# The seam between the mixing and the last part: image 0's spectra loaded early, its last two columns copied from evicted tiles, and a fixed order

## The chip, the cores and the metric

The kernel runs on one core of a Trainium2 chip. The metric is the device time of one launch in microseconds (us), the median of several runs. Engines are named as in the profile: PE (matmuls), PEld (PE's weight loads), DVE (vector), ACT (scalar), POOL (GpSimd) and SP (the sync engine, which here only issues DMAs). A trailing q, as in SPq, is the part of an engine that issues DMAs.

## What is computed

All data is float32. The input is 32 images of 128 channels, 64 x 64 pixels. A convolution in a learned transform domain comes first, then attention over channels and a mixture of experts on the pixels as tokens. Cut to what matters:

```python
x = x + conv(group_norm(x))
# conv: x_f = tensor_product(x)            butterflies along h and w, complex
#       prod = einsum('bihw,oihw->bohw', x_f, w_f)
#       out = real(tensor_product_inverse(prod))
t = tokens(x)                              # 4096 tokens of 128 channels per image
t = t + attn(layer_norm(t))                # softmax of a 128 x 128 channel Gram matrix
t = t + moe(layer_norm(t))                 # 8 experts, top 2, gates renormalised
x = from_tokens(t)
```

## The kernel before

The work has three parts, one after another.

Part one (lines 163 to 563) goes over the 32 images: group norm, and the two butterflies as matmuls with 64 x 64 matrices. Its results, the spectra, go to the DRAM tile `xf`.

Part two (lines 566 to 757), the mixing, goes over the 64 columns w of the spectrum. For each w, SP loads the column of all images and input channels in four tiles `l` (pool `lp`, a ring of 8), POOL spreads them into the tile `s` (lines 600 and 602), PE makes the weights' spectrum `g` from `wst` (line 632), ACT and DVE bring it to `f` (643), and PE multiplies `s` with `f` (654, the tiles `m`). ACT and DVE evict `m` into one of two tiles `o`, one for each half of the 64 + 64 output channels (`mix_out`, line 664; its last argument hh picks ACT or DVE, and the DVE copy comes after the ACT one). `store` (line 673) writes a half of column w into the DRAM tile `pf`, in eight DMAs of 128 KB on SP. A tile `o` holds column w in the partitions of w % 2, so after the last column it holds columns 62 and 63.

Part three (lines 763 to 1390) goes over the images again. For image b, eight tiles `r` (pool `rp`, a ring of 10) are loaded from `pf`, each with 16 output channels, all 64 columns, real part in partitions 0 to 63 and imaginary part in 64 to 127 (`load_r`, line 856: two DMAs of 256 KB). PE applies the inverse transform along w. For the first two images this is done in 16 pieces per image (`pw`, line 920, evicted by ACT into `u` at 927), for the later ones in eight (`pu`, 877). Then follows the inverse along h (`pz`, 939, or `py`, 899), which DVE adds to the image `y` (947 or 907), which is loaded from the input again. Then come the transposition to tokens (`pt`, 1021), layer norm, attention and experts (`pe`, 1296), and the store. In the steady state the steps of three images overlap.

The order of the instructions on each engine comes from a planner (`Plan`, line 25): each operation is given an engine, an estimated duration, a due time, what it follows and which buffers of a ring it takes and frees. The planner plays this through and then emits the operations in the order it found. Within `tc.manual_schedule()` that order is kept; the code between the second and the third planner's run (lines 763 to 797: pools, loads of constants, clearing `rank`) is outside of it, and the framework's own scheduler places it. When a pool's memory is taken over by a new pool, a tile in it waits for what used that memory before.

At the seam of parts two and three the third part's list `first` is emitted ahead of its planner's operations: `prepare` (line 799), which folds a mean into the expert weights, the attention weights and the router's column sums by four PE products (804, 812, 820) with DVE work behind each, and then `load_r` of image 0 for e = 0 and 1 on POOL and for e = 2 and 3 on ACT. `prepare` reads `wkv`, `prx` and `kvb`, which ACT's queue loads (lines 774 to 797). The other four tiles `r` of image 0 and its image `y` are loaded on SP.

Of the kernel before, what the change touches and what calls it, by code (L numbers as in the profile page):

```python
# [10 lines left out]
F32 = mybir.dt.float32  # L11
# [3 lines left out]
PSUM = bass.MemoryType.PSUM  # L15

P = 128
HW = 64
NPIX = HW * HW
NT = NPIX // P  # L20
NE = 8
# [69 lines left out]
def kernel(  # L91
# [15 lines left out]
    nc = tc.nc  # L107
    B = x.shape[0]
    xv = x.rearrange("b c h w -> b c (h w)")
# [3 lines left out]
    n = HW  # L113
# [6 lines left out]
    pf = dram.tile([n, n, P * n], F32, name="pf")  # L120
# [35 lines left out]
    nc.gpsimd.memset(mhalf, -0.5)  # L156

    wctx = ctx.enter_context(ExitStack())
    wstp = wctx.enter_context(tc.tile_pool(name="wstp", bufs=1))
    wst = wstp.tile([P, 32, P], F32, name="wst")  # L160


    with ExitStack() as ph1:
        pp = ph1.enter_context(tc.tile_pool(name="pp1", bufs=4, space=PSUM))
        xp = ph1.enter_context(tc.tile_pool(name="xp1", bufs=3))
        st = ph1.enter_context(tc.tile_pool(name="st1", bufs=1))
# [19 lines left out]
        lo, hi = slice(0, n), slice(n, P)  # L186
# [244 lines left out]
        def store(b, g):  # L431
            def run():
                f = tile_of.pop(("f", b, g))

                for k in range(0, 8, 4):
                    nc.sync.dma_start(xf[b, :, 8 * g + k : 8 * g + k + 4, :], f[:, k : k + 4])
            return run
# [125 lines left out]
            plan.run()  # L563


    with ExitStack() as ph2:
        gp = ph2.enter_context(tc.tile_pool(name="gp", bufs=2, space=PSUM))
        mp = ph2.enter_context(tc.tile_pool(name="mp", bufs=2, space=PSUM))
        lp = ph2.enter_context(tc.tile_pool(name="lp", bufs=8))
        sp = ph2.enter_context(tc.tile_pool(name="sp", bufs=2))  # L570
        wf = ph2.enter_context(tc.tile_pool(name="wf", bufs=2))
        op = ph2.enter_context(tc.tile_pool(name="op", bufs=1))
# [95 lines left out]

        def store(w, half):

            for c in range(0, n, 8):
                lo = (half * n + c) * n
                nc.sync.dma_start(
                    pf[w, :, lo : lo + 8 * n], outs[half][w % 2 * n : w % 2 * n + n, c : c + 8].rearrange("m o h -> m (o h)")
                )

        rest = []
# [21 lines left out]
        def mixed(*after):  # L699

            while rest:
                w, half, g, at = rest.pop()
                add(
                    ("mo", w, half, g, 1), "DVE", 1.25, at + 0.1, lambda: mix_out(w, half, g, 1),
                    [("mo", w, half, g, 0), *after], (), ("m",),
                )
                if g:
                    add(
                        ("st", w, half), "SP", 0.1, at + 0.2, lambda: store(w, half),
                        [("mo", w, half, g, hh) for g in range(2) for hh in range(2)], (), ("o",), 8.0,  # L710
                    )

# [50 lines left out]
    eps = ctx.enter_context(tc.tile_pool(name="eps", bufs=3, space=PSUM))  # L763
    cps = ctx.enter_context(tc.tile_pool(name="cps", bufs=1, space=PSUM))
    tps = ctx.enter_context(tc.tile_pool(name="tps", bufs=3, space=PSUM))
    rp = ctx.enter_context(tc.tile_pool(name="rp", bufs=10))
    xp = ctx.enter_context(tc.tile_pool(name="xp", bufs=2))
    st = ctx.enter_context(tc.tile_pool(name="st", bufs=1))
    up = ctx.enter_context(tc.tile_pool(name="up", bufs=1))
    wp = ctx.enter_context(tc.tile_pool(name="wp", bufs=2))  # L770
    pfv = pf.rearrange("w (r b) (e m) -> b e r w m", r=2, e=8)
    ct = ctx.enter_context(tc.tile_pool(name="ct", bufs=1))
    wkv = ct.tile([P, 2, P], F32, name="wkv")
    nc.scalar.dma_start(wkv[:, 0, :], wkT)
    nc.scalar.dma_start(wkv[:, 1, :], wvT)
    rb_sb = ct.tile([P, NE], F32, name="rb_sb")
    nc.scalar.dma_start(rb_sb, router_b.partition_broadcast(P))


    rank = ct.tile([P, NE], F32, name="rank")  # L780
# [6 lines left out]
    QX = P + 2 * NE  # L787
    prx = [ct.tile([P, QX], F32, name=f"prx{i}") for i in range(2)]
    for t in prx:
        nc.scalar.dma_start(t[:, P + NE : QX], router_w)  # L790
    rws = ct.tile([P, NE], F32, name="rws")

    tk = [ct.tile([P, NT, P], F32, name=f"tk{i}") for i in range(2)]
    u = up.tile([P, n, P], F32, name="u")
    kvb = ct.tile([P, 2, P], F32, name="kvb")
    nc.scalar.dma_start(kvb[:, 0, :], bk.partition_broadcast(P))
    nc.scalar.dma_start(kvb[:, 1, :], bv.partition_broadcast(P))

    def prepare():

# [41 lines left out]
            engine, us, SLOT * at, run, [made[k] for k in names if k[0] >= 0], take, free, late  # L842
        )

    xs, rs, tile_of, first = {}, {}, {}, [prepare]

    def transfers(b):
        def load_x():
            xs[b] = xp.tile([P, HW, HW], F32, tag="x", name=f"y{b}")
            nc.sync.dma_start(xs[b].rearrange("c h w -> c (h w)"), xv[b])  # L850

        def load_r(e, queue=nc.sync):
            def run():
                t = rs[b, e] = rp.tile([P, 16 * n], F32, tag="r", name=f"r{b}_{e}")
                for r in range(2):
                    queue.dma_start(t[r * n : (r + 1) * n], pfv[b, e, r])
            return run

        if b == 0:

            first.extend(load_r(e, nc.gpsimd if e < 2 else nc.scalar) for e in range(4))

        for e in range(8):
            early = b == 0 and e < 4
            add(
                b, f"r{e}", "SP", 0.2, b - 0.5 + 0.08 * e, (lambda: None) if early else load_r(e), take=("r",),
                late=0.0 if early else 5.0,
            )
        add(b, "x", "SP", 0.1, b + 0.2, load_x, take=("x",), late=12.0)

    def conv(b):
        def w_inverse(e):
# [71 lines left out]
        def h_out_piece(q):  # L944
            def run():
                acc = xs[b][:, :, 8 * q : 8 * q + 8]
                nc.vector.tensor_tensor(
                    acc, tile_of.pop(("cz", b, q)).rearrange("o (w h) -> o h w", h=n), acc, ALU.add
                )
            return run  # L950

        if b < 2:
            for e in range(8):
                at = b + 0.08 * e
                for oh in range(2):
                    add(
                        b, f"w{e}_{oh}", "PE", 0.95, at + 0.04 * oh, w_inverse_piece(e, oh),
                        [f"r{e}"] + [(b - 1, f"h{k}") for k in range(4)], ("pe",), ("r",) if oh else (),
                    )
                    add(  # L960
                        b, f"wo{e}_{oh}", "ACT", 0.65, at + 0.04 * oh, w_out_piece(e, oh), [f"w{e}_{oh}"], (), ("pe",),
                    )
            for g in range(4):
                for k in range(2):
                    at = b + 0.68 + 0.07 * g + 0.035 * k
                    h, ho = (f"h{g}", f"ho{g}") if k else (f"h{g}_0", f"ho{g}_0")
                    add(
                        b, h, "PE", 1.05, at, h_inverse_piece(2 * g + k),
                        [f"wo{e}_{oh}" for e in range(8) for oh in range(2)] + ([f"h{g}_0"] if k else []), ("pe",),
                    )  # L970
# [411 lines left out]
    for b in range(B):  # L1382
# [1 line left out]
        conv(b)  # L1384
        front(b)
        experts(b)
    with tc.manual_schedule():
        for run in first:
            run()
        plan.run()  # L1390


# [51 lines left out]
```

## Time and profile before

| | |
|---|---|
| three runs | 6056.81, 6056.97, 6062.2 us; median 6056.97 |
| span of the profiled execution | 6062.4 us (0.2 above the highest of the three runs; 5.4 above the median) |
| busy: PE, PEld | 5891.6 us (97%), 4677.6 us (77%) |
| busy: DVE, ACT, POOL | 4221.2 us (70%), 3756.5 us (62%), 4191.0 us (69%) |
| part one, part two, part three | to about 931, 931 to 2537, from 2537 us on |
| one image in the steady state of part three | 106.4 us |
| instructions fetched | queue q8: 749 packets, 12.27 MB |
| time to landing: `pf<-o`, `r<-pf` on SP, POOL, ACT | 3.3, 4.7, 7.3, 10.7 us (medians) |

A line of the timeline has the start and the length in us, the engine, the line of the kernel, the operation with the tiles it writes and reads, the count, and in brackets the idle time of the engine ahead of it with what ended that. "issue" means that the engine waited for nothing that the profile shows. The chain of waits goes back from the last instruction of the kernel, at each step to what released it. A line of the table by stretches has the stretch, its length, and the busy time (with the number of instructions) of PE, PEld, DVE, ACT and POOL, then the clock granted to PE as a share of the full one, the busy share of the 16 DMA engines and what they moved in GB/s.

### The profile page before, as it was taken

What the parts mean: (1) busy time and instruction counts of PE and PEld (TensorE: products, weight loads), DVE (VectorE), ACT (ScalarE), POOL (GpSimd) and SP (SyncE); (2) the same over time, 40 slices, a digit from 0 to 9 for tenths busy, and PEclk for the clock granted to TensorE, in tenths of its full rate; (3) what the DMA queues carried; (4) which work ended last, traced back from release to release, by engine and by line L of the source; (5) the groups of instructions that cost most, each with busy time, mean ns of one, the idle gap of its engine ahead of it and who ended that gap; (6) DMA issues with size and microseconds to landing.
All of it is one profiled execution on the core that took longest, in us unless ns stands there. A gap on an engine that the chain in (4) does not pass through costs nothing.

```text
span 6062.4 us, 219265 instructions
## 1 busy us (share of the span) xinstructions
PE 5891.6 (97%) x95372; PEld 4677.6 (77%) x95372; DVE 4221.2 (70%) x7696; ACT 3756.5 (62%) x7057; POOL 4191.0 (69%) x3765
## 2 busy tenths in 40 slices
PE   7999999999999999889999999999999999999998
PEld 7999999999999999776666666666666666666654
DVE  5565545555555555448878787787878878787878
ACT  7666664555555555366667667666766766676663
POOL 2110006666666666428898898989989898998988
PEclk9999999999999999999999999999999999999999
DMA  6767666666666666632313222231322223132100
GB/s 200 238 224 237 234 214 193 172 173 172 172 174 171 171 171 172 160 107 77 92 56 102 67 88 81 72 97 57 101 68 84 84 64 104 57 97 71 65 27 28
DMA packets 555044, 756.74 MB, mean 125 GB/s; under 512 B 58592, under 2 KB 319712, under 8 KB 549984
## 3 DMA queue, kind: packets, MB, share of 16 engines
q1 hardware_dynamic: 551856, 738.76, 41.0%
q8 instruction: 749, 12.27, 0.9%
q0 software_dynamic: 896, 2.62, 0.1%
q14 instruction: 215, 1.76, 0.1%
q10 hardware_dynamic: 1328, 1.32, 0.1%
HBM read 406.93 MB, written 335.54 MB: 122 GB/s over the span
## 4 chain that ended last, share of the span: by engine, by line
PE 88%; ACT 7%; issue 2%; DVE 1%; POOL 1%; DMA 1%; SPq 0%; ACTq 0%; POOLq 0%; DVEq 0%
PE pe L1296 28%; PE m L654 17%; PE g L632 9%; PE pf L418 7%; PE pu L877 6%; PE pp L1145 4%; PE py L899 4%; PE pg L1072 4%; PE pv L396 3%; PE px L1283 2%; ACT xn L1273 2%; ACT u L887 2%; PE pz L373 1%; PE pt L1021 1%; ACT z L383 1%
## 5 line engine op out<-in xcount | busy, mean ns | idle before, releaser
L1296 PE MATMUL pe<-ew_sb,xT 128*128 128x512 f32 x4096 | 1948.4, 597 | 18.6 <-DVE tm L1307 15.1
L1307 DVE TENSOR_TENSOR tm<-pe,oh 128x512 f32<-128x512 f32 x2028 | 1346.6, 684 | 478.9 <-PE pe L1296 456.6
L1332 POOL TENSOR_TENSOR tm<-tm 128x512 f32<-128x512 f32 x1014 | 1285.0, 1284 | 202.6 <-DVE tm L1307 199.3
L1296 PEld LDWEIGHTS pe<-ew_sb,xT 128*128 128x128 f32 x4096 | 701.6, 191 | 523.4 <-issue 400.1
L643 DVE COPY f<-g 128x1024 f32<-128x1024 f32 x508 | 622.3, 1225 | 644.4 <-PE g L632 644.2
L654 PE MATMUL m<-f,s 128*64 128x64 f32 x32768 | 1068.9, 224 | 1.1 <-ACT f L643 0.8
L654 PEld LDWEIGHTS m<-f,s 128*64 128x64 f32 x32768 | 999.0, 138 | 62.4 <-issue 1.5
L600 POOL COPY s<-l 128x512 f32<-128x512 f32 x512 | 547.2, 1105 | 526.4 <-issue 509.7
L643 ACT COPY f<-g 128x1024 f32<-128x1024 f32 x508 | 514.7, 1013 | 556.4 <-PE g L632 530.1
L1335 POOL TENSOR_TENSOR tk<-tk,tm 128x256 f32<-128x256 f32 x1014 | 753.9, 743 | 79.5
L1333 POOL TENSOR_TENSOR tm<-tm 128x512 f32<-128x512 f32 x507 | 650.3, 1283 | 39.8
L887 ACT COPY u<-pu 64x512 f32<-64x512 f32 x960 | 556.3, 579 | 135.1 <-PE pu L877 121.6
L632 PE MATMUL g<-c,wst 9*128 9x128 f32 x16256 | 599.6, 283 | 1.7 <-issue 1.5
L632 PEld LDWEIGHTS g<-c,wst 9*128 9x128 f32 x16256 | 503.0, 186 | 36.2 <-issue 1.5
L349 POOL TENSOR_TENSOR grstd<-gms,mhalf 128x1 f32<-128x1 f32 x32 | 17.8, 555 | 737.8 <-DVE gms L345 737.8
L1158 ACT ACTIVATE pp<-pp,m 128x128 f32<-128x128 f32 x1024 | 440.9, 431 | 124.2 <-PE pp L1145 99.2
L602 POOL TENSOR_SCALAR s<-l 128x512 f32<-128x512 f32 x256 | 511.3, 1997 | 0.0
L877 PEld LDWEIGHTS pu<-qw,r 128*128 128x128 f32 x3840 | 455.1, 193 | 62.8 <-ACT u L887 49.0
L877 PE MATMUL pu<-qw,r 128*128 128x128 f32 x3840 | 475.8, 277 | 25.1 <-ACT u L887 25.1
L1289 ACT COPY xT<-px 128x512 f32<-128x512 f32 x256 | 150.2, 587 | 563.2 <-PE px L1283 560.1
L418 PE MATMUL pf<-ph,v 128*128 128x128 f32 x4096 | 491.2, 278 | 6.2 <-issue 1.4
L418 PEld LDWEIGHTS pf<-ph,v 128*128 128x128 f32 x4096 | 467.0, 192 | 16.0 <-ACT z L383 7.1
(169 smaller groups left out, 8569.6 us busy)
## 6 DMA issues: line engine op xcount, KB each, us to landing
xf<-f SPq DMA_DIRECT2D x512, 256.0 KB, 3.3
pf<-o SPq DMA_DIRECT2D x1024, 128.0 KB, 3.3
l<-xf SPq DMA_DIRECT2D x1012, 128.0 KB, 3.2
r<-pf SPq DMA_DIRECT2D x504, 256.0 KB, 4.7
x<-in_x_dram SPq DMA_DIRECT2D x256, 256.0 KB, 4.5
y<-in_x_dram SPq DMA_DIRECT2D x32, 2048.0 KB, 9.3
out_dram<-so SPq DMA_DIRECT2D x256, 256.0 KB, 2.2
tw<-in_tw_dram SPq DMA_DIRECT2D x6, 384.0 KB, 7.5
```

Source lines behind the costliest of these rows:

```text
L418: nc.tensor.matmul(pl[:, j * P : (j + 1) * P], vs[b][:, 8 * g + j, :], ph.rearrange("h r m -> h (r m)"), start=True, stop=True,)
L600: nc.gpsimd.tensor_copy(dst, src)
L632: nc.tensor.matmul(pg[g // 2][:, g % 2, m * P : (m + 1) * P], wst[rows, 16 * half + 4 * t + m, :], c[rows].rearrange("r h k -> r (h k)"), ...
L643: copy(f.rearrange("i m (g o) -> i m g o", g=2), tile_of["g", w, half, t][k].rearrange("i g (o m) -> i m g o", o=4))
L654: nc.tensor.matmul(ps[hh * n : (hh + 1) * n, q, :], s[:, h].rearrange("i k b -> i (k b)")[:, B * r : B * r + n], f[:, h, r, :], start=(r = ...
L877: nc.tensor.matmul(ps[:, k, :], rs[b, e][:, k * P : (k + 1) * P], qw.rearrange("w r m -> w (r m)"), start=True, stop=True,)
L887: nc.scalar.copy(u[r * n : (r + 1) * n, :, oh * n + 8 * e : oh * n + 8 * e + 8], ps[oh * n : (oh + 1) * n, :, r * n : (r + 1) * n].rearran ...
L1296: nc.tensor.matmul(ps, tile_of["xT", b, i // 4][:, i % 4, :], ew_sb[:, es, :].rearrange("d e c -> d (e c)"), start=True, stop=True,)
L1307: nc.vector.tensor_tensor(tile_of["tm", b, i // 2][:, i % 2, es, :], tile_of.pop(("pe", b, i, half)).rearrange("p (e c) -> p e c", c=P), t ...
L1332: nc.gpsimd.tensor_tensor(tm[:, k, 0:4, :], tm[:, k, 0:4, :], tm[:, k, 4:8, :], ALU.add)
L1333: nc.gpsimd.tensor_tensor(tm[:, :, 0:2, :], tm[:, :, 0:2, :], tm[:, :, 2:4, :], ALU.add)
L1335: nc.gpsimd.tensor_tensor(t[:, lo : lo + 2, :], t[:, lo : lo + 2, :], tm[:, :, m, :], ALU.add)
```

## The change

- The ring of part three's tiles `r` is opened ahead of part two (pool `rp`, now 8 tiles) and serves part two as the ring of the tiles `l` too; two more tiles come from a pool `rp2` in part three. Tile i = 8b + e lies in `rp` where i % 10 < 8.
- At the end of part two POOL loads rows 0 to 61 of all eight tiles `r` of image 0 from `pf` (`first_rows`: 16 DMAs of 62 rows of 4 KB). They follow the stores of column 61 and POOL's last spread.
- Rows 62 and 63 of each half come from the tiles `o` in SBUF (`last_rows`: 16 DMAs of two rows on SP), when the halves of columns 62 and 63 are evicted; all 16 stand on SP ahead of the store of the second half of column 63.
- The store of the first half of column 63 goes from SP to POOL. Behind it on POOL stand the load of image 0's `y`, all loads of constants (from ACT) and the clearing of `rank`.
- `prepare` becomes an operation of the third planner, behind the last `pz` of image 0; on PE its four products come between the last `pz` and the first `pt`, and on DVE its six instructions come ahead of the last addition to `y` of image 0. The first pieces `pw` of image 1 come later among the `pt` of image 0: the first stood ahead of all of them and comes behind the fifth.
- The fixed order spans everything from part two on. The pools of part three reuse memory with waits by tile, and their order is changed; `wst` and the constants lie on the other side of the memory.

Apart from this, the order of the instructions on each engine is the same in both kernels.

```diff
-    wstp = wctx.enter_context(tc.tile_pool(name="wstp", bufs=1))
+    wstp = wctx.enter_context(tc.tile_pool(name="wstp", bufs=1, side="right"))
...
+    rp = ctx.enter_context(tc.tile_pool(name="rp", bufs=8))
+    pfv = pf.rearrange("w (r b) (e m) -> b e r w m", r=2, e=8)
+    ctx.enter_context(tc.manual_schedule())
+    rs = {}
     with ExitStack() as ph2:
...
-        lp = ph2.enter_context(tc.tile_pool(name="lp", bufs=8))
...
-            t = tile_of["l", w, j] = lp.tile([P, NB, 2, n], F32, tag="l", name=f"l{w}_{j}")
+            t = rp.tile([P, 16 * n], F32, tag="r", name=f"l{w}_{j}")
+            t = tile_of["l", w, j] = t.rearrange("i (b r h) -> i b r h", b=NB, r=2)
...
         def store(w, half):
+            queue = nc.gpsimd if (w, half) == (n - 1, 0) else nc.sync
...
+        def first_rows(e):
+            t = rs[0, e] = rp.tile([P, 16 * n], F32, tag="r", name=f"r0_{e}")
+            for r in range(2):
+                nc.gpsimd.dma_start(t[r * n : r * n + n - 2], pfv[0, e, r][0 : n - 2])
+
+        def last_rows(e):
+            half, lo = e // 4, 16 * (e % 4)
+            for r in range(2):
+                nc.sync.dma_start(
+                    rs[0, e][r * n + n - 2 : r * n + n],
+                    outs[half][B * r : B * r + n + 1 : n, lo : lo + 16].rearrange("m o h -> m (o h)"),
+                )
...
+        for e in range(8):
+            half = e // 4
+            add(("r", e), "POOL", 1.2, n - 0.9 + 0.01 * e, lambda e=e: first_rows(e), [("st", n - 3, 0), ("st", n - 3, 1), ("s", n - 1, 3, 2)], ("l",))
+            add(
+                ("rl", e), "SP", 0.4, n - 1 + 0.5 * half + 0.01 * e, lambda e=e: last_rows(e),
+                [("r", e)] + [("mo", w, half, g, hh) for w in (n - 2, n - 1) for g in range(2) for hh in range(2)],
+            )
+        plan.run()
...
+    def pool(name, bufs, **kw):
+        return ctx.enter_context(tc.tile_pool(name=name, bufs=bufs, reuse_waits="tile", **kw))
...
+    rp2 = pool("rp2", 2)
...
+    kc = pool("kc", 1, side="right")
+    xs, tile_of = {}, {}
+    xs[0] = xp.tile([P, HW, HW], F32, tag="x", name="y0")
+    nc.gpsimd.dma_start(xs[0].rearrange("c h w -> c (h w)"), xv[0])
+    wkv = kc.tile([P, 2, P], F32, name="wkv")
+    nc.gpsimd.dma_start(wkv[:, 0, :], wkT)
...
-        def load_r(e, queue=nc.sync):
-            def run():
-                t = rs[b, e] = rp.tile([P, 16 * n], F32, tag="r", name=f"r{b}_{e}")
+        def load_r(e):
+            def run():
+                i = 8 * b + e
+                ring, tag = (rp, "r") if i % 10 < 8 else (rp2, "r2")
+                t = rs[b, e] = ring.tile([P, 16 * n], F32, tag=tag, name=f"r{b}_{e}")
                 for r in range(2):
-                    queue.dma_start(t[r * n : (r + 1) * n], pfv[b, e, r])
-            return run
-
-        if b == 0:
-            first.extend(load_r(e, nc.gpsimd if e < 2 else nc.scalar) for e in range(4))
+                    nc.sync.dma_start(t[r * n : (r + 1) * n], pfv[b, e, r])
+            return run
...
+            if b == 0:
+                add(b, "prep", "PE", 3.5, 0.98, prepare, ["h3"], ("pe",), ("pe",))
...
-    with tc.manual_schedule():
-        for run in first:
-            run()
-        plan.run()
+    plan.run()
```

More of the change, by code (lines that the diff above doesn't have):

```diff
@@ L669, in store @@
         def store(w, half):
+            queue = nc.gpsimd if (w, half) == (n - 1, 0) else nc.sync
             for c in range(0, n, 8):
                 lo = (half * n + c) * n
+                queue.dma_start(
+                    pf[w, :, lo : lo + 8 * n], outs[half][w % 2 * n : w % 2 * n + n, c : c + 8].rearrange("m o h -> m (o h)")
+                )
[6 more added lines that the diff above has]
+            for r in range(2):
                 nc.sync.dma_start(
-                    pf[w, :, lo : lo + 8 * n], outs[half][w % 2 * n : w % 2 * n + n, c : c + 8].rearrange("m o h -> m (o h)")
+                    rs[0, e][r * n + n - 2 : r * n + n],
+                    outs[half][B * r : B * r + n + 1 : n, lo : lo + 16].rearrange("m o h -> m (o h)"),
                 )
@@ L708, in mixed @@
                     add(
-                        ("st", w, half), "SP", 0.1, at + 0.2, lambda: store(w, half),
+                        ("st", w, half), "POOL" if (w, half) == (n - 1, 0) else "SP", 0.1, at + 0.2, lambda: store(w, half),
                         [("mo", w, half, g, hh) for g in range(2) for hh in range(2)], (), ("o",), 8.0,
@@ L755 @@
             mixed()
-        with tc.manual_schedule():
-            plan.run()
-    wctx.close()
[L763 to L780, printed above, removed]
+        for e in range(8):
[5 more added lines that the diff above has]
+            )
@@ new lines @@
+        plan.run()
+    wctx.close()
+    def pool(name, bufs, **kw):
+        return ctx.enter_context(tc.tile_pool(name=name, bufs=bufs, reuse_waits="tile", **kw))
+    eps = pool("eps", 3, space=PSUM)
+    cps = pool("cps", 1, space=PSUM)
+    tps = pool("tps", 3, space=PSUM)
+    xp = pool("xp", 2)
+    up = pool("up", 1)
+    rp2 = pool("rp2", 2)
+    ct = pool("ct", 1)
+    st = pool("st", 1)
+    wp = pool("wp", 2)
+    kc = pool("kc", 1, side="right")
+    xs, tile_of = {}, {}
+    xs[0] = xp.tile([P, HW, HW], F32, tag="x", name="y0")
@@ L781 @@
+    nc.gpsimd.dma_start(xs[0].rearrange("c h w -> c (h w)"), xv[0])
+    wkv = kc.tile([P, 2, P], F32, name="wkv")
+    nc.gpsimd.dma_start(wkv[:, 0, :], wkT)
+    nc.gpsimd.dma_start(wkv[:, 1, :], wvT)
+    rb_sb = kc.tile([P, NE], F32, name="rb_sb")
+    nc.gpsimd.dma_start(rb_sb, router_b.partition_broadcast(P))
+    rank = kc.tile([P, NE], F32, name="rank")
     for e in range(NE):
@@ L784 @@
     NG = 4
-    xg = [ct.tile([P, 4, P], F32, name=f"xg{i}") for i in range(NG)]
[L787 to L797, printed above, removed]
+    QX = P + 2 * NE
+    prx = [kc.tile([P, QX], F32, name=f"prx{i}") for i in range(2)]
+    for t in prx:
+        nc.gpsimd.dma_start(t[:, P + NE : QX], router_w)
+    rws = kc.tile([P, NE], F32, name="rws")
+    kvb = kc.tile([P, 2, P], F32, name="kvb")
+    nc.gpsimd.dma_start(kvb[:, 0, :], bk.partition_broadcast(P))
+    nc.gpsimd.dma_start(kvb[:, 1, :], bv.partition_broadcast(P))
+    u = up.tile([P, n, P], F32, name="u")
+    tk = [ct.tile([P, NT, P], F32, name=f"tk{i}") for i in range(2)]
+    xg = [ct.tile([P, 4, P], F32, name=f"xg{i}") for i in range(NG)]
     def prepare():
@@ L843, in add @@
         )
-    xs, rs, tile_of, first = {}, {}, {}, [prepare]
     def transfers(b):
@@ L850, in load_x @@
             nc.sync.dma_start(xs[b].rearrange("c h w -> c (h w)"), xv[b])
-        def load_r(e, queue=nc.sync):
+        def load_r(e):
             def run():
-                t = rs[b, e] = rp.tile([P, 16 * n], F32, tag="r", name=f"r{b}_{e}")
+                i = 8 * b + e
+                ring, tag = (rp, "r") if i % 10 < 8 else (rp2, "r2")
+                t = rs[b, e] = ring.tile([P, 16 * n], F32, tag=tag, name=f"r{b}_{e}")
                 for r in range(2):
-                    queue.dma_start(t[r * n : (r + 1) * n], pfv[b, e, r])
+                    nc.sync.dma_start(t[r * n : (r + 1) * n], pfv[b, e, r])
             return run
-        if b == 0:
-            first.extend(load_r(e, nc.gpsimd if e < 2 else nc.scalar) for e in range(4))
         for e in range(8):
-            early = b == 0 and e < 4
             add(
-                b, f"r{e}", "SP", 0.2, b - 0.5 + 0.08 * e, (lambda: None) if early else load_r(e), take=("r",),
-                late=0.0 if early else 5.0,
+                b, f"r{e}", "SP", 0.2, b - 0.5 + 0.08 * e, load_r(e) if b else (lambda: None), take=("r",),
+                late=5.0 if b else 0.0,
             )
-        add(b, "x", "SP", 0.1, b + 0.2, load_x, take=("x",), late=12.0)
+        add(b, "x", "SP", 0.1, b + 0.2, load_x if b else (lambda: None), take=("x",), late=12.0 if b else 0.0)
     def conv(b):
@@ L1386 @@
         experts(b)
-    with tc.manual_schedule():
-        for run in first:
-            run()
-        plan.run()
+    plan.run()
 def arrange(inputs):
```

## The prediction

> **What bounds the kernel now.** I read the page first, for its busy table by slices, then the chain of waits between 2500 and 2800 us, the timeline of the same stretch, and the busy table of single stretches there. The page says that TensorE is busy 97% of the span, so only the places where it isn't can be won. Between the first and the last slice, PE falls to 8 tenths only in two, from 2425 to 2728, and in the middle of these the chain leaves PE altogether:
>
> ```profile
> 2527.27 2.04 PE m L654 x64
> 2529.33 1.01 ACT o L664
> 2530.36 1.24 DVE o L664
> 2533.40 3.36 DMA pf<-o
> 2537.28 5.01 DMA r<-pf
> 2543.56 11.26 DMA r<-pf
> 2554.83 3.09 DMA pf<-o
> 2560.38 3.45 DMA kvb<-in_bk_dram
> 2563.83 1.17 PE pmk L812 x2
> 2565.23 9.54 PE pw L920 x268
> 2574.77 3.64 issue
> ```
>
> Start, length, what: from 2533 to 2564 the end of the kernel hangs on transfers alone: the last columns go to `pf` in DRAM, come back as `r` (image 0's spectra), and behind them in the queues stand the constants that `prepare` needs. The timeline shows the queues:
>
> ```profile
> 2506.08 2.04 POOL L602 TENSOR_SCALAR s<-l 128x512 f32<-128x512 f32 x1
> ...
> 2535.09 1.16 POOL L856 DMA_DIRECT2D r<-pf  x2 [26.98 <-DMA pf<-o]
> ...
> 2542.28 1.00 ACT L664 COPY o<-m 64x1024 f32<-64x1024 f32 x1 [8.22 <-DMA r<-pf]
> ...
> 2544.57 10.71 SPq L673 DMA_DIRECT2D pf<-o  x8
> 2555.38 12.15 SPq L856 DMA_DIRECT2D r<-pf  x10
> ...
> 2563.81 1.19 PE L812 MATMUL pmk<-wkv,om 128*128 128x256 f32 x2 [25.15 <-DMA kvb<-in_bk_dram]
> ```
>
> To be seen: POOL has nothing to do from 2508.1 on; the last eviction (L664 on ACT) waits 8.22 us although its matmuls ended at 2536.75, because a transfer of `r` stands ahead of it on ACT; and PE waits 25.15 us at L812 while the first spectra are already there. The table of stretches (PE busy, then granted clock, DMA share, GB/s at the end) shows what follows:
>
> ```profile
> 2536.75:2565.16 28.41, 3.26 (x9) 1.78 (x9) 3.83 (x4) 1.00 (x1) 1.32 (x10) 0.58 0.87 241
> 2565.16:2604.20 39.04, 28.43 (x776) 27.79 (x777) 5.77 (x10) 9.38 (x16) 0.00 (x0) 0.87 0.85 223
> 2584.00:2587.00 3.00, 0.00 (x0) 0.00 (x0) 0.00 (x0) 0.19 (x1) 0.00 (x0) 1.00 1.04 249
> ```
>
> So two losses: 28.4 us without work, and 39 us for the 24 pieces `pw` and `pz` of image 0, in which PE stops three times (3.64, 3.16 and 3.07 us) with no releaser, each time with the DMA engines full (share 1.04).
>
> **What the Trainium skill says.** (1) "Runtime: NRT & Kernel Launch", section "Instruction fetch mechanics": instructions come by DMA in blocks of 16 KiB, 256 of them. The page agrees: its queue q8 moved 12.27 MB in 749 packets, 16.4 KB each, and the three stops lie about 128 matmuls and 128 weight loads apart. It calls the fetch mostly hidden; here it seems not to be when the DMA engines are full, so I take the stops as late fetches (inferred, no row names them). (2) "TensorE: Matmul & The Clock Gate", Part 1: an idle array falls to half clock. Agrees: 0.50 from 2542 to 2568. (3) "DMA: Bandwidth & Descriptors", "Why a DMA increments its semaphore by 16 and not by 1": a transfer is spread over the largest number of engines up to 16 that divides its rows, on POOL taken in rotation, though some POOL copies were seen on 16 anyway. For the change's 62 rows that would be 2. No row of before shows such a shape.
>
> **The change part by part**, against the profiled execution (span 6062.4 us; that is 0.2 above the highest of the three times and 5.4 above their median, 6056.97; I carry the difference over to the median).
>
> *First 62 rows early.* Sixteen POOL transfers of 254 KB move from 2535 and later to 2508.1, when POOL's last spread ends. They need the stores of columns up to 61; those are issued until about 2501. Issue: 16 x 0.53 us (POOL row `r<-pf`) = 8.5 us, with one wait of about 7.3 us (its time to landing), since the second eight need the counters of the first. Bytes: 4.06 MB, with 2 MB of column stores beside them, at the 250 to 330 GB/s seen from 2540 to 2596: 18 to 24 us. So they land by about 2530, ahead of 2536.75. Cost: none on POOL, which is idle to 2535; if that cover were gone, `pw` would wait. But PE is mixing, and uses a block of instructions per 4.2 us (96 matmuls in 3.12). Full DMA slowed that to 8.6 and 7.9 us per block (2578.4, 2587.0, 2594.9) and, near 2620, to 5.3. The first stop came 5 to 6.6 us after the engines filled. That leaves about 13 us at risk: 13 x (1 - 4.2/5.3) = 3 to 13 x (1 - 4.2/8) = 6 us lost; nothing if POOL's queue leaves room. I take **3**, ends 0 and 7.
>
> *Last two rows from SBUF.* Sixteen SP transfers of 8 KB, 0.45 to 0.6 us each. The first eight follow the eviction that ends at 2531.6: issued by 2536, landing after 3.3 us (page) and so before each is due. The other eight need the last eviction. PE ends at 2536.75, ACT 1.0, DVE 1.25: about 2539.1, as nothing stands ahead of it on ACT now. Landing of the first of them: 2539.1 + 1.0 + 3.3 = 2543.4, against the ninth piece at 2536.8 + 8 x 0.93 = 2544.2. Cost 0, at worst some 3 us with full engines. Behind these on SP stand the last column's second half, r1 and y1; none is needed for 20 us.
>
> *Store of column 63, first half, to POOL; y0, constants behind it.* Eight issues from 2531.6, 4.4 us. y0 (2 MB) then starts at about 2537 as before (2537.68). Its POOL issue has no row: between 0.53 (SP) and 8 x 0.53 = 4.2 us by size; 2 taken. The transfer took 13.8 or 15.0 us, so it lands by 2552 to 2556; the first DVE addition comes at 2553 or later. Constants by 2550, due at 2560. Cost 0, ends 0 and 4. ACT loses 11 DMA issues: no cost, and the 8.22 us wait goes.
>
> *`prepare` moved behind `pz`.* PE need not wait for constants before `pw` (the 25.15 us go). New cost on the chain: its DVE work 2 x 0.69 + 1.22 + 2 x 0.42 + 0.16 = 3.6, the first matmul 1.0, and the last addition to y0, now behind it: **5** us.
>
> *Moved pools, SP ring of 8 + 2.* Reuse waits by tile; the order on every engine is otherwise as before. 0.
>
> Sum to the first transposition of y0, `pt`. Before: 2605.06, less the 1.08 us of one `pw` piece that now comes later: 2604.0. After, undisturbed: 2536.75 + 16 x 0.93 (`pw`) + 0.65 (last copy) + 8 x 0.93 (`pz`) + 5 = 2564.7. Gain 39.3. Then the fetch losses. `pw` and `pz` took 39.0 us where 23 would do: 16 lost (9.9 stops, 6 half clock). Afterwards PE arrives warm, but 11 MB (stores 2, y0 and y1 4, r1 and the next two 5) at 250 to 330 GB/s take 33 to 44 us, so the same six blocks run with full engines: I take **12**, from 6 (two stops) to 17 (five). Gain 39.3 - 3 - 12 = **24.3 us**. What is late next is PE's own instruction supply. Everything behind `pt` is unchanged at 106.4 us an image: it only moves earlier.
>
> **Rivals.**
> *A, as above*: gains 13 to 31, most likely 24: 6056.97 - 24.3 = 6032.7. For it: the stops with full engines. Chance 0.62.
> *B, no fetch losses of weight*: gains 31 to 41, about 37, 6020. For it: near 2620 a full stretch cost only 1.05 + 1.35 us. Against: three stops of over 3 us in just these pieces. Chance 0.18.
> *C, the transfers collide*: y0, the stores and r1 crowd one stretch, the early rows slow the mixing by 7, and `pw` waits for its last rows: 39.3 - 7 - 17 - 3 - 4 = 8 us, 6049, within 0.2%. Chance 0.11.
> *D, slower: 62 rows on two engines, always the same two*. Sixteen engines move 250 to 330 GB/s, two 31 to 41: 4.06 MB take 99 to 131 us from 2508, and the last spectra land at 2607 to 2639, where today their piece begins at about 2589. Loss 18 to 50, about 6085. It decides below 4.06 MB / (2589 - 2508 us) = 50 GB/s, three engines. Against it: the skill's rotation spreads eight such transfers over all 16. Chance 0.09.
>
> **How the numbers follow.** The forecast is A's 6032.7. A and B hold 0.80, from 6016 to 6044; adding half of C gives 6016 to 6050. 0.2%, 12 us, is about what a measurement can tell from no change. Faster by more: A and B and a little of C, 0.82; within: 0.09; slower: D, 0.09.
>
> **What would show it.** In the changed profile: POOL transfers `r<-pf` from about 2508; PE's mixing ending by 2540 with stops of 0 to 7 us; `pw` following within 2 us at full clock; no wait at `pmk`; stops without releaser in `pw` and `pz` with the DMA share near 1; `pt` at about 2580. I am wrong if `pw` waits for `r` or `y` for more than 5 us, if the mixing stops for more than 7, or if the images behind no longer take 106.4.

## The result, and the profile after

The changed kernel takes 6039.05 us (median of six runs, 6034.45 to 6041.73), the kernel before 6058.51 us (six runs beside it): ratio 0.9966, with a 95% interval of 0.9955 to 0.9978, so about 20 us are won. The profiled execution is the fastest of the six; its span is 6032.7 us.

The chain of waits (start, length, what) no longer leaves TensorE for 31 us between the parts:

```profile
2527.15 9.51 PE m L658 x320
...
2536.68 1.01 ACT o L668
...
2539.53 8.13 DMA r<-o
...
2547.79 0.80 PE pw L946 x20
```

The only transfer ahead of `pw` is now the copy of the last two rows, and it costs little, as the timeline of TensorE in the same stretch shows (start, length, line, tiles, count, idle time ahead):

```profile
2505.66 1.96 PE L658 MATMUL m<-f,s 128*64 128x64 f32 x58
2508.31 0.45 PE L658 MATMUL m<-f,s 128*64 128x64 f32 x6 [0.68 <-issue]
...
2511.80 1.15 PE L636 MATMUL g<-c,wst 9*128 9x128 f32 x26
2515.07 0.53 PE L636 MATMUL g<-c,wst 9*128 9x128 f32 x6 [2.11 <-issue]
2515.53 3.56 PE L658 MATMUL m<-f,s 128*64 128x64 f32 x64
...
2536.47 4.60 PE L946 MATMUL pw<-qw,r 128*64 128x64 f32 x150
2543.41 1.44 PE L946 MATMUL pw<-qw,r 128*64 128x64 f32 x42 [2.35 <-issue]
2545.40 2.08 PE L946 MATMUL pw<-qw,r 128*64 128x64 f32 x64 [0.55 <-DMA r<-o]
...
2564.18 3.48 PE L965 MATMUL pz<-hm,u 128*64 128x64 f32 x111 [2.66 <-issue]
...
2573.08 4.07 PE L1049 MATMUL pt<-ident,y 128*128 128x128 f32 x20 [2.33 <-DVE y L973]
```

`pw` starts when the mixing ends, at 2536.47 us, and `pmk` waits for no constant. The 25 us wait is gone. What is new stands in the mixing: it stops with no releaser at 2507.6 and 2513.0 us (and for 0.40 us at 2521.2), and the 64 matmuls behind the second stop take 3.56 us instead of the 2.08 they take at full clock. The busy table by stretches gives the size (busy time of PE first, near the end the granted clock, the DMA share and GB/s); first the changed kernel from the eighth-last `g` to the last, and its `pw` and `pz`:

```profile
2498.32:2525.98 27.66, 24.46 (x676) 22.64 (x673) 12.84 (x11) 11.11 (x11) 12.09 (x19) 0.94 0.70 221
2536.47:2567.66 31.19, 24.20 (x775) 23.24 (x771) 6.07 (x8) 10.39 (x17) 4.00 (x16) 1.00 0.84 237
```

and the mixing's stretch in the kernel before:

```profile
2504.22:2526.09 21.87, 21.87 (x676) 20.55 (x672) 12.85 (x11) 11.11 (x11) 3.90 (x3) 1.00 0.37 86
```

The same 676 matmuls take 27.66 us instead of 21.87: 5.8 us are paid in the mixing, with the DMA share at 0.70 instead of 0.37. `pw` and `pz` take 31.2 us where the kernel before took 39.0.

The start of that stretch also differs, 2498.3 against 2504.2 us, although the order up to there is the same. So spans of single executions mislead here. For all that follows I cut each profile at six points of TensorE's timeline: A, the eighth-last `g`; the last `g`; the first `pw`; the end of image 0's last `pz`; the first `pt`; and the first `pb` of the attention, behind which nothing of the change is left. All columns are us.

| kernel | A | to last `g` | to `pw` | `pw`, `pz` | to `pt` | to `pb` | A to `pb` | rest of span |
|---|---|---|---|---|---|---|---|---|
| before | 2504.2 | 21.9 | 39.1 | 38.8 | 1.1 | 33.0 | **133.8** | 3424.4 |
| before, second profile | 2500.7 | 21.8 | 40.0 | 39.4 | 1.1 | 32.9 | **135.2** | 3427.1 |
| after | 2498.3 | 27.7 | 10.5 | 31.1 | 5.5 | 36.9 | **111.6** | 3422.8 |
| after, second | 2505.3 | 30.5 | 10.5 | 31.6 | 5.5 | 35.4 | **113.4** | 3424.7 |
| after, third | 2499.1 | 27.4 | 10.5 | 37.5 | 5.5 | 34.8 | **115.7** | 3422.2 |
| e1 early loads paced | 2505.4 | 25.7 | 12.5 | 34.0 | 5.5 | 36.4 | **114.1** | 3424.3 |
| e2 y1 later | 2507.8 | 27.9 | 10.5 | 33.9 | 5.5 | 37.6 | **115.4** | 3424.7 |
| e3 `prepare` later | 2504.0 | 30.0 | 10.5 | 33.9 | 4.3 | 36.6 | **115.4** | 3422.3 |
| e4 order only | 2500.4 | 21.8 | 14.9 | 50.9 | 5.5 | 36.0 | **129.2** | 3423.6 |
| e7 no y0, y1 | 2502.2 | 32.4 | 10.7 | 28.9 | 5.6 | 35.2 | **112.7** | 3424.5 |
| e8 paced, `prepare` behind y | 2500.4 | 27.9 | 12.0 | 34.5 | 3.1 | 35.9 | **113.4** | 3423.6 |
| e9 no copy | 2502.5 | 30.5 | 16.7 | 37.5 | 5.5 | 33.6 | **123.7** | 3424.8 |
| e10 zero rows, no y0, y1 | 2502.4 | 21.8 | 10.5 | 32.1 | 5.6 | 36.1 | **106.0** | 3423.7 |

A lies anywhere in 2498 to 2508 us, in kernels with the same order up to there; the rest behind `pb` agrees within 5 us. The seam itself differs by 134.5 - 113.6 = 20.9 us (means of two and three profiles). That is the change, as far as single profiles tell it; the medians, 19.5 us apart here and 16.4 in a second series further down, have 1 to 5 us less, and where these lie stays open.

### The profile page after: what moved, and what is told of

It reads as the page before. It is cut to its first block, busy times and chain, and to the rows that moved or that the text cites. A ratio compares the mean times of both kernels' runs of the same rounds, so it can differ in the third digit from the quotient of the medians.

```text
span 6032.7 us, 219314 instructions
## 1 busy us (share of the span) xinstructions
PE 5884.8 (98%) x95372; PEld 4672.1 (77%) x95372; DVE 4220.6 (70%) x7696; ACT 3757.1 (62%) x7057; POOL 4205.9 (70%) x3793
## 4 chain that ended last, share of the span: by engine, by line
PE 88%; ACT 7%; issue 2%; DVE 1%; POOL 1%; DMA 1%; SPq 0%; POOLq 0%; ACTq 0%; DVEq 0%
PE pe L1324 28%; PE m L658 17%; PE g L636 9%; PE pf L418 7%; PE pu L903 6%; PE pp L1173 4%; PE py L925 4%; PE pg L1100 4%; PE pv L396 3%; PE px L1311 2%; ACT xn L1301 2%; ACT u L913 2%; PE pz L373 1%; ACT z L383 1%; PE pt L1049 1%
```

## The theory and its rivals

Theory: the queue order and the early rows took away the 28 us without work; what is left at the seam is TensorE's instruction supply, late whenever the DMA engines are full. Rivals: the stops are waits for data or buffers; or they belong to the clock or to new code; or the gain came from the new order (constants, `prepare`, the eviction) and not from the early rows.

Two things speak for the theory ahead of any experiment. The first is where the stops stand. In the timeline above, 6 + 32 + 64 + 26 = 128 pairs of matmul and weight load lie between the first stop and the second. In the other profiles whose mixing stops at the seam, the stops fall on the same borders or further ones 128 pairs on: after 58 of the 64 matmuls of a piece, then after 26 of the 32 of a `g`, then after 26 of a piece. Data waits would fall at the start of a piece.

The second is the fetches themselves: the traces hold every packet of the instruction queue q8 with its start and length. The 749 packets of the changed kernel (16.4 KB each) stand beside 95,372 matmuls, 95,372 weight loads and 1,059 semaphore instructions of TensorE, so each brings a block of 256 instructions, or 128 pairs. Counted off in order, each block has its packet.

Between 2495 and 2640 us of all 14 profiles, and in the mixing of e5 below, there are 113 stops of 0.25 us or more without a releaser. Every one lies at the border of two blocks, and ends 1.2 to 1.65 us (median 1.42) after the new block's packet has landed. Where TensorE passes a border without a stop, the packet landed at least 1.2 us ahead. In the changed kernel's mixing from 1000 to 2495 us a packet starts 0.6 us after TensorE enters the block before it, takes 1.1 us, and lands 2.4 us ahead of its own border (medians). Ahead of the three stops in the first profile's mixing it started 2.7, 4.3 and 4.1 us after. So the stops are late fetches; what makes a fetch late is a question for the experiments.

## Experiments

**The two parts of the change, alone.** e4 keeps the order and drops the early rows:

```diff
-            queue = nc.gpsimd if (w, half) == (n - 1, 0) else nc.sync
+            queue = nc.sync
...
-                nc.gpsimd.dma_start(t[r * n : r * n + n - 2], pfv[0, e, r][0 : n - 2])
+                nc.gpsimd.dma_start(t[r * n : r * n + n], pfv[0, e, r])
...
-            add(("r", e), "POOL", 1.2, n - 0.9 + 0.01 * e, lambda e=e: first_rows(e), [("st", n - 3, 0), ("st", n - 3, 1), ("s", n - 1, 3, 2)], ("l",))
-            add(
-                ("rl", e), "SP", 0.4, n - 1 + 0.5 * half + 0.01 * e, lambda e=e: last_rows(e),
...
+            add(("r", e), "POOL", 1.2, n - 0.9 + 0.01 * e, lambda e=e: first_rows(e), [("st", n - 1, half), ("s", n - 1, 3, 2)], ("l",))
```

> The order of the changed kernel (constants and y0 behind the stores on POOL, preparation behind h3, no loads on ScalarE), but no early rows: all 64 rows of image 0's spectra are loaded on POOL once the last column's stores are issued, with no copy from the evicted tiles. Theory (the gain is from early loading, its price the fetch stops in the mixing): the mixing's last stretch is back at 22 us, 5.8 us won; PE then stands still for 8 to 12 us waiting for the store and the load behind it and starts cold; 6 to 10 us slower than the changed kernel, near 6046 us. Rival (the gain came from the order alone: constants, preparation, the eviction that no longer waits): the same time as the changed kernel within 2 us, near 6039 us.

Measured: 6053.82 us (21 runs) beside 6061.28 of before, ratio 0.9989 (0.9982 to 0.9995). The mixing is back at 21.8 us without a stop, and the seam has 129.2 us. Its timeline of TensorE shows waits that name the load, piece after piece:

```profile
2537.18 6.20 PE L942 MATMUL pw<-qw,r 128*64 128x64 f32 x128 [4.22 <-DMA r<-pf]
...
2561.33 3.68 PE L942 MATMUL pw<-qw,r 128*64 128x64 f32 x64 [5.35 <-DMA r<-pf]
```

The order alone is worth 5 us of the seam (134.5 to 129.2) or 7.5 us of the median; the rival that it is everything falls. Theory's 8 to 12 us of waiting were too few: the seven `pw` waits add to 16.6 us, and the time is well above the 6046 us expected. Not all of it belongs to the order: y0 stands behind all these loads on POOL in e4, and VectorE's first addition waits for it, which holds `pz` up for 3.68 us.

e9 keeps the early rows and drops the copies from the evicted tiles:

```diff
-                    rs[0, e][r * n + n - 2 : r * n + n],
-                    outs[half][B * r : B * r + n + 1 : n, lo : lo + 16].rearrange("m o h -> m (o h)"),
+                    rs[0, e][r * n + n - 2 : r * n + n], pfv[0, e, r][n - 2 : n]
...
-                [("r", e)] + [("mo", w, half, g, hh)
+                [("r", e), ("st", n - 1, half)] + [("mo", w, half, g, hh)
```

> One part of the change undone: the last two rows of each of image 0's spectra are read back from pf behind the stores of the last column, on the same SP queue and in the same place, instead of copied from the evicted tiles; the early rows stay. Theory: the first pw can't start before the store has landed and its two rows are read, so TensorE stands for 6 to 10 us with a wait that names a DMA between the mixing and pw, at half clock behind it, and the second half's store is a second wait of 0 to 4 us; the stretch from the eighth-last g to the first pb is 119 to 125 us. Rival (the early rows alone bring the gain, since the fetch stops in pw would have taken that time anyway): less than 2 us over the changed kernel's 111.6 to 113.4 us.

Measured: 6050.3 us beside 6062.76, ratio 0.9978 (0.9968 to 0.9987); the seam 123.7 us, as expected. One line of its timeline has the price, a wait and 150 matmuls in 6.36 us that take 4.60 in the changed kernel:

```profile
2549.66 6.36 PE L945 MATMUL pw<-qw,r 128*64 128x64 f32 x150 [6.01 <-DMA r<-pf]
```

So the seam goes from 134.5 us to 129.2 with the order, to 123.7 with the early rows, to 113.6 with the copies (the middle two from one profile each). By these seams half of the gain is the 16 small copies that spare the last rows the round trip through DRAM. The medians give them less: beside before, e9 gains 12.5 us and the changed kernel 19.5 and 16.4 in two other series, so 4 to 7 us; against the one run of the changed kernel in e9's own series (6038.73 us) it is 11.6. A fifth to a half of the gain is what the record supports.

**Is it the traffic?** e5 puts the suspected cause where nothing depends on it:

```diff
+    spare = dram.tile([8, P, 16 * 2 * n], F32, name="spare")
+    def burst(lo):
+        for i in range(lo, lo + 4):
+            nc.sync.dma_start(spare[i], xf[i, :, 0:16, :].rearrange("c w m -> c (w m)"))
...
+        add(("burst",), "SP", 0.4, 30.0, lambda: burst(0), [("st", 29, 0)])
...
+        if b == 10:
+            add(b, "burst", "SP", 0.4, b + 0.5, lambda: burst(4), ["h0"])
```

> Adds two bursts of copies that the reference does not ask for: four transfers of 1 MB each from the input to a spare tensor, that nothing reads and nothing waits for, on SP's queue; one in the mixing at column 30, one in the last part at image 10. In both places the kernel is otherwise that of the changed one. Theory (PE's instruction fetch is late while the DMA engines are full, and it hurts where PE runs through 128 pairs of small matmul and weight load in 4.2 us): in the mixing 2 to 4 stops of 0.5 to 3.5 us without a releaser, always after 128 pairs from the one before, 2 to 8 us in all; at image 10, where the matmuls are longer and far fewer a us, no more than 1 us. Rival (the stops at the seam are waits for data or buffers): no stop without a releaser in either place; only the mixing's own loads, which queue behind on SP, can be late, and then the wait names a DMA.

Measured: 6053.42 us (one run). In its timeline of TensorE, in the middle of the mixing:

```profile
1701.28 0.71 PE L642 MATMUL g<-c,wst 9*128 9x128 f32 x10
1703.54 0.94 PE L642 MATMUL g<-c,wst 9*128 9x128 f32 x22 [1.55 <-issue]
1704.41 3.60 PE L664 MATMUL m<-f,s 128*64 128x64 f32 x64
...
1711.32 3.25 PE L664 MATMUL m<-f,s 128*64 128x64 f32 x54 [1.71 <-issue]
```

and in the table by stretches, the burst in the mixing and the one at image 10:

```profile
1699.00:1714.50 15.50, 12.23 (x269) 11.29 (x266) 6.13 (x5) 4.92 (x7) 9.73 (x9) 0.78 0.88 277
3545.00:3555.00 10.00, 10.00 (x152) 6.50 (x148) 6.45 (x10) 4.17 (x11) 9.77 (x6) 1.00 1.01 347
```

Two stops without a releaser, 3.3 us in all, and some 3 us of half clock behind them; between them 22 + 64 + 32 + 10 = 128 pairs. At image 10 the engines are as full (1.01), and TensorE is busy for the whole 10 us: there it issued 152 matmuls in 10 us, where the mixing issues some 300. Only two borders of blocks lie in this burst, but the first shows why it is free: its block lasts 8.2 us, so the next packet, which starts 3.4 us after TensorE enters it, still lands 3.9 us ahead. Ahead of the two stops in the mixing the packets started 3.7 and 5.5 us after, in blocks that last 4.2 us undisturbed. Traffic that has no tie to TensorE's data stops it, at block borders, where it runs through instructions fast. The rivals of data and of new code fall here, and so does the clock: it drops behind the stops, not ahead of them.

e10 goes the other way and takes traffic out of the seam (e7 the same for the residuals alone):

```diff
-    nc.gpsimd.dma_start(xs[0].rearrange("c h w -> c (h w)"), xv[0])
+    nc.gpsimd.memset(xs[0], 0.0)
...
-            nc.sync.dma_start(xs[b].rearrange("c h w -> c (h w)"), xv[b])
+            if b == 1:
+                nc.gpsimd.memset(xs[b], 0.0)
+            else:
+                nc.sync.dma_start(xs[b].rearrange("c h w -> c (h w)"), xv[b])
...
-            for r in range(2):
-                nc.gpsimd.dma_start(t[r * n : r * n + n - 2], pfv[0, e, r][0 : n - 2])
+            nc.gpsimd.memset(t, 0.0)
```

(e7 has the first two parts, e10 all three.)

> Leaves work out: the residuals y0 and y1 are set to zero on POOL instead of loaded, so 4 MB less go through the DMA engines between 2536 and 2568 us; the order on every engine stays. Theory: pw and pz of image 0, 31 to 34 us in four profiles and 23 us if nothing stopped them, come down to 25 to 28 us, and the stops that remain lie where image 1's spectra are loaded; the run is 4 to 8 us under the changed kernel. Rival (the stops belong to the matmul sequence itself or to PE's first pass through new code, whatever the traffic): pw and pz stay at 31 to 34 us.

> Leaves work out: the 62 early rows of image 0's spectra and the residuals y0 and y1 are set to zero on POOL instead of loaded, 8 MB less for the DMA engines at the seam; every engine's order stays, and so do the stores, the copies of the last two rows and image 1's spectra. Theory: the mixing's stretch is back at 21.9 us without a stop; pw and pz have no stop of over 1 us until image 1's spectra are loaded into freed buffers, 24 to 28 us; from the eighth-last g to the first pb 99 to 105 us. Rival (new code and not traffic stops TensorE): the stops stay at the same instructions with the same lengths, and the stretch has its 112 to 114 us, as it nearly did without the residuals alone (112.7).

Measured, e7: 6040.16 us beside 6062.49 (ratio 0.9966, 0.9952 to 0.998), `pw` and `pz` 28.9 us, seam 112.7: its mixing, which has nothing to do with y, was the slowest of all (32.4 us), and in this profile took back what `pw` and `pz` gained. Over all runs the gain is there: the changed kernel took 6046.11 us in the same series, 6 us more, which is what was expected. Measured, e10: 6033.83 us (one run), mixing 21.8 us without a stop, seam 106.0; but `pw` and `pz` 32.1 us instead of 24 to 28. Its table by stretches, cut where the loads of image 1's spectra begin, tells why:

```profile
2534.74:2546.60 11.86, 11.86 (x409) 11.81 (x406) 1.23 (x1) 7.90 (x13) 10.53 (x17) 1.00 0.53 118
2546.60:2566.79 20.19, 13.12 (x369) 12.59 (x365) 4.84 (x7) 2.49 (x5) 0.00 (x0) 0.92 0.95 264
```

The first 409 matmuls run without a stop at a mean DMA share of 0.53; from 2547 us SP issues image 1's `r`, the share is 0.95, and the timeline has three stops in 20 us:

```profile
2547.97 3.37 PE L948 MATMUL pw<-qw,r 128*64 128x64 f32 x109 [1.29 <-issue]
...
2554.57 3.95 PE L967 MATMUL pz<-hm,u 128*64 128x64 f32 x128 [1.86 <-issue]
2561.88 4.97 PE L967 MATMUL pz<-hm,u 128*64 128x64 f32 x110 [3.36 <-issue]
```

The first of them begins at 2546.7 us, just ahead of these loads: its packet started at 2545.6, while the last column's stores filled the engines (share 0.87 and 0.75 from 2542 to 2546). The other two, 5.2 us, come with the loads. The theory holds, and my expectation of the time didn't: I had put the late stops down to y0 and y1. Without them SP's next loads start earlier, 12.3 us behind the first `pw` instead of 15 to 17, with no y1 between them, and fill the engines.

**Can the loss be avoided?** Four variants try to move it. e1 spreads the early loads with an idle instruction behind each pair:

```diff
+            nc.gpsimd.tensor_tensor(idle[:, 0:10], om[:, 0:10], mhalf[:, 0:10], ALU.pow)
```

> The 16 early transfers of image 0's spectra are issued with a POOL instruction of about 1.75 us between each pair, so they are spread over some 22 us instead of 15; order, buffers and everything else as in the changed kernel. Theory (what is left at the seam is PE's instruction fetch, late whenever the DMA engines are full): the stretch from the eighth-last g to the end of the mixing, 27.7 us in the changed kernel and 21.9 us before, comes down to 22 to 24 us, the DMA share there below 0.9, and the run is 3 to 5 us under the changed kernel. Rival (the stops wait for data or buffers): the stretch keeps 27 to 28 us or gets longer, since every transfer lands later. Rival (the clock): half-speed matmuls stay where they were, at about 2515 us, whatever the transfers do.

Measured: 6045.05 us beside 6061.28, ratio 0.9969 (0.9956 to 0.9981). The mixing's stretch falls to 25.7 us, not to 22 to 24, and stops follow later in the mixing and in `pw`:

```profile
2530.69 0.45 PE L659 MATMUL m<-f,s 128*64 128x64 f32 x6 [1.02 <-issue]
...
2551.95 12.32 PE L948 MATMUL pw<-qw,r 128*64 128x64 f32 x362 [3.36 <-issue]
```

Its seam, 114.1 us, is that of the changed kernel (111.6 to 115.7). No gain that one profile could tell. The same bytes cross the same dense stretch, which fits, though this run alone doesn't show it to be the reason.

e2 loads y1 behind image 1's spectra:

```diff
-        add(b, "x", "SP", 0.1, b + 0.2, load_x if b else (lambda: None), take=("x",), late=12.0 if b else 0.0)
+        add(b, "x", "SP", 0.1, b + 0.2, load_x if b > 1 else (lambda: None), take=("x",), late=12.0 if b else 0.0)
...
+                if (b, e) == (1, 7):
+                    load_x()
```

> The 2 MB load of image 1's residual (y1) is issued behind image 1's last spectra instead of ahead of its second ones; every engine's order is otherwise that of the changed kernel. Theory: 2 MB less go through the DMA engines between 2554 and 2568 us, so of the 8 us that pw and pz of image 0 lose, the later stop (2.7 us near 2562) shrinks or goes; but the load then meets pt and pw1 of the next stretch, which already lost 3.4 us. In all 0 to 3 us gained, and the stops move with the traffic. Rival (stops are waits for data): pw and pz of image 0 need none of y1, so nothing moves, and the time is the changed kernel's within 1 us.

Measured: 6045.3 us beside 6061.28, ratio 0.9975 (0.9965 to 0.9984); seam 115.4. `pw` and `pz` have 33.9 us, and the stop ahead of the last `pz` is 3.76 us long: not shorter. SP goes straight on with image 1's spectra in y1's place (16 transfers issued from 2563 to 2578 us), and as in e10 these keep the engines full (share 1.04 from 2570 to 2576 us).

e3 moves `prepare` far back, e8 just behind the last addition to y (with e1's pacing):

```diff
-                add(b, "prep", "PE", 3.5, 0.98, prepare, ["h3"], ("pe",), ("pe",))
...
+        if b == 0:
+            add(b, "prep", "PE", 3.5, s1, prepare, ["na"], ("pe",), ("pe",))
```

> The four small matmuls of the preparation (pm, pmk, pms) and their VectorE work go behind image 0's normalisation step instead of ahead of its pz; all else as in the changed kernel. My step said that the preparation costs 5 us on the chain between the last pz and pt (5.4 us stand there in the changed kernel's trace, with 2.3 us of waiting for VectorE's y). If VectorE's extra work is what holds y back: the stretch from the end of pz to pt falls from 5.4 to 1 to 3 us and the run is 2 to 4 us under the changed kernel. Rival: the 5.4 us are the ordinary length of the residual's last pieces, or the work comes back where it now stands (its products wkv are needed by pb), and the time is the same within 1 us.

```diff
-                add(b, "prep", "PE", 3.5, 0.98, prepare, ["h3"], ("pe",), ("pe",))
+                add(b, "prep", "PE", 3.5, 0.98, prepare, ["ho3"], ("pe",), ("pe",))
```

> The early transfers paced as in the first series, and the preparation's matmuls behind the last piece of the residual in the order, so that VectorE's y is no longer held back: pt follows the last pz after 1 to 2 us instead of 5.4, the preparation's 3.1 us of TensorE then stand behind the first three pt, in all 2 us gained from the preparation (the 2.3 us wait for y goes), and 2 to 4 us in the mixing. From the eighth-last g to the first pb 110 to 112 us, against 114.1 with the pacing alone; the time 2 to 4 us under the changed kernel on this chip, which the medians can hardly tell. Rival: the wait only moves, to the first xg or to pb, and the stretch keeps its 114 us.

Measured, e3: 6044.35 us beside 6061.28, ratio 0.9972 (0.9962 to 0.9982). `pt` follows the last `pz` after 4.3 us, of which 2.5 are a stop; `prepare` itself, now behind the last `pw` piece, takes 5.65 us from its first matmul to the first `pg`, since three waits for VectorE of 0.78, 0.78 and 0.89 us lie in it. The work came back where it stands; the rival was right. Measured, e8: 6043.88 us beside 6062.49, ratio 0.9971 (0.9961 to 0.9982). VectorE's y is no longer waited for, and `pt` comes 3.1 us behind the last `pz`, of which 1.72 are a stop. The seam is 113.4 us: the wait is won and no difference is left that the stops' own spread wouldn't hide.

**How far one profile can be trusted.** The changed kernel was run twice more and the kernel before once.

> The changed kernel once more, unaltered, beside the others on the same chip, for a second profile of the seam. From the eighth-last g to the first pb the first profile had 111.6 us (133.8 in the kernel before), and the three variants of the first series 114.1 (early transfers paced), 115.4 (y1 later) and 115.4 (preparation later). If the first profile was an ordinary one, 111 to 113 us again, and each variant was a loss of 2 to 4 us; if the fetch stops of one and the same program differ by some us from execution to execution, 114 to 116 us, and pacing gained 1 to 2 us while the other two were worth nothing.

> The changed kernel, unaltered, for a third profile: the same stretch had 111.6 and 113.4 us, its mixing part 27.7 and 30.5 us, pw and pz 31.1 and 31.6 us. If fetch stops vary only in where they fall, 111 to 115 us again with the stops at the same instructions.

> The kernel before, unaltered, for a second profile of its seam. From the eighth-last g to the first pb the first profile had 133.8 us. If the seam's time is a property of the program, 132 to 136 us again, whatever the span is; what the spans differ by then lies ahead of the eighth-last g, where both kernels run the same order.

Measured: 6046.11 us beside 6062.49, ratio 0.9974 (0.9965 to 0.9983); 6038.73 us; 6064.58 us. The seam had 113.4, 115.7 and 135.2 us. The stops in the mixing stand at the same instructions each time, with 0.68, 1.32 and 0.95 us for the first and 2.11, 2.39 and 1.84 for the second. e5, whose seam is the changed kernel's own, is a fourth profile of it: 116.4 us (which makes the difference of the means 20.2 us instead of 20.9), and 3424.7 us behind `pb`, with no trace of the second burst. So pacing gained nothing, and e2 and e3 lost nothing that these profiles can tell: all lie in the range of the changed kernel, 111.6 to 116.4 us.

## Why the prediction was right, step by step

Forecast 6032.7 us, a gain of 24.3; measured 6039.05, a gain of 19.5 beside it (16.4 in the second series). The mechanism, A, was right, and the size 5 to 8 us too good. By its terms, with three profiles of the changed kernel and two of before:

- **Undisturbed gain to `pt`, 39.3 us.** From A to `pt` before took 100.8 and 102.3 us, less 1.1 for the piece that moved; after, 74.8, 78.1 and 80.9. The means differ by 22.6 us; with the losses measured below put back (6.6 + 10.4) that makes 39.6. Right: no wait at `pmk`, `pw` in the same instant as the mixing's end and at full clock.
- **Last two rows, cost 0 to 3.** 0.85, 0.77 and 0 us of waits for `r<-o`. The eviction ended at 2538.96 as reckoned (2539.1), but a copy took 8.1 us to land instead of 3.3, with the DMA share at 0.85 from 2538 to 2543, beside y0 and the constants. A stop of 2.35 us in `pw` just ahead of it probably hid part of that. POOL's second eight early transfers waited 6.5 us in all; 7.3 were reckoned.
- **y0, constants, stores, POOL: cost 0.** Right: the first addition to y waits for `pz`, not for y0. y0's issue, for which I took 2 us, needs 0.56.
- **Mixing slowed, 3 us from 0 to 7.** 5.8, 8.6 and 5.5 us, mean 6.6. This term was mis-sized. The 13 us at risk were about right: in the first profile the engines are full from 2508 to 2520 us. But two blocks take 6.8 and 6.5 us there instead of 4.2, where the 3 us rested on 5.3. The stops alone come to 3.2, 3.7 and 2.8 us, under the 7 named as a sign of being wrong; the rest, 2.6 of the 5.8 us in the first profile, is half clock behind a stop, which I had not reckoned here at all. With it the mixing lost 8.6 us once, more than the term's upper end.
- **Stops in `pw` and `pz`, 12 us from 6 to 17.** 8.1, 8.6 and 14.5 us over the 23 undisturbed, the waits for the last rows included, mean 10.4. Right, and 1.6 us under the term, which by luck pays for part of what the mixing lost.
- **`prepare`, 5 us.** 5.5 in all three profiles. Right; 2.3 of them are the wait for VectorE's y.
- **Nothing behind `pt` changes.** Not quite: from `pt` to `pb` 36.9, 35.4 and 34.8 us against 34.0 (with the moved piece), mean 1.7 lost. The stops in image 1's `pw` add to 3.0 to 3.3 us instead of 2.3 to 2.4, and part of `pt` runs at half clock after the wait for y (20 matmuls in 4.07 us; in e9 in 2.52). Behind `pb` all profiles agree, so the images did stay as they were.

The sum with the measured terms: 39.6 - 6.6 - 10.4 - 1.7 = 20.9 us. Of the rivals, D is out (POOL's queue moved the 62 rows at 250 GB/s, five times what D turns on), B too (17 us of fetch losses), and C has one of its parts: the mixing lost as much as C had said.

That the stops are late instruction fetches was inferred in the prediction, since no row of the timeline names a fetch; the packets of q8 show it. That full DMA engines make the fetches late is shown by e5 and e10. How a packet comes to start late (whether it stands behind data in an engine's own queue) no record shows. The Trainium skill ("Runtime: NRT & Kernel Launch", "Instruction fetch mechanics") has blocks of that size and calls their fetch mostly hidden; here it is not, where PE needs a block every 4.2 us and the data queues fill the engines.

## What to carry to other kernels

A round trip through DRAM at a seam is best broken in two: load early what is already there, and copy the last piece from where it still lies in SBUF; here the early rows were worth some 5 us and the copies 4 to 12. But early loads are not free even on idle queues: if TensorE runs through short matmuls beside them, price its instruction supply, with the half clock behind each stop. Here pacing and reordering such transfers only moved the stops; in e2 and e10 the next loads in the queue filled what was freed. A stretch with long matmuls is worth a try: e5's burst cost nothing there.

## What was not expected of the hardware

- Transfers of 62 rows on POOL filled the engines: over 5 us their queue alone took 0.68 of the 16 engines' time and moved 250 GB/s; with the column's stores beside them it was 1.04 and 373 GB/s. The skill's divisor rule ("DMA: Bandwidth & Descriptors", "Why a DMA increments its semaphore by 16 and not by 1") gives such a transfer two engines (though some POOL copies were seen on 16), and takes them in rotation on POOL, so that a series can still cover all 16. That fits; how many engines a single one used no run shows.
- After a stop of 1.55 us in e5 and 2.11 us in the changed kernel the clock fell to half (64 matmuls in 3.6 us instead of 2.08); after stops of 2.35 and 2.66 us in `pw` and `pz` of the changed kernel it did not. In its third profile half clock did follow a stop of 2.10 us in `pz` (0.50 granted from 2560.8 to 2563 us). What decides stays open.
- The same program reaches the seam at 2498 to 2508 us, while the 3420 us behind it differ by 5 us at most. Where the first 2500 us vary wasn't looked into.
